# Moving the drive scalings from GpSimd to VectorE, the sine arguments to GpSimd, and splitting two more stores, in a two-layer convolution kernel on one core

## The chip, the core and the metric

The kernel runs on one core of a Trainium2 chip. The core has a matrix engine (TensorE; PE in the profile, with its weight loads as PEld), VectorE (DVE), ScalarE (ACT), GpSimd (POOL) and SyncE (SP), which here only issues DMAs. Each engine works through its own list of instructions in order. All DMAs run on 16 shared DMA engines. DMAs are issued from SP, from ACT (at the start) and from POOL.

The metric is the device time in microseconds. Before the change it is 9159.09 us, the median of three runs from 9153.91 to 9171.87.

## The reference

The input `x` is 8 x 8 x 512 x 512 (batch elements, channels, rows, columns), float32. Two layers are added to it.

```python
# layer 0: spectral convolution of the group-normalised input
x = x + _L0_conv_ref(_gn(x), T, X, weights1_ri, weights2_ri)
#   every second row and column -> rfft2 -> the 4+4 x 4 lowest modes mixed
#   over channels by w1, w2 -> sum with exp(lam * X), exp(lam * T) back to 512 x 512

# layer 1, on v = _gn(x)
grid = drive = v
for _ in range(15):
    mapped = 3.9 * grid * (1.0 - grid)
    local = conv3x3_per_channel(mapped, K_local)
    grid = 0.85 * (0.7 * mapped + 0.3 * local) + 0.15 * drive
cml = clip(grid, 0.0001, 0.9999)
nca = sigmoid(conv1x1(relu(conv3x3(v, Wp, bp)), Wu, bu))     # 8 -> 128 -> 8 channels
gin = concatenate([v, cml, nca])
g   = sigmoid(conv1x1(relu(conv3x3(gin, Wg1, bg1)), Wg2, bg2))
x   = x + g * cml + (1.0 - g) * nca
```

The **drive** is the term `0.15 * drive` in the loop of 15 steps. The sines and cosines of layer 0 are computed in the kernel from `X` and `T`.

## The kernel before

**Planes and slabs.** For each element the normalised input is written to a plane `xn` in DRAM. The 15 steps run on slabs of it: a set (class `Slabs`) holds four channels of four slabs of 32 rows that overlap, as one tile of 128 partitions by 4 x 512. A set loads two drive tiles of that size, `dE` (index 0) and `dO` (index 1), which hold the same rows in two arrangements, since a step turns channels and slabs about. Even steps add `dE`, odd ones `dO`. An element has two halves of four sets each (channels 0 to 3 and 4 to 7), and the second half has a fifth set, the `Tail`. These are two phases of 15 steps: 60 and 75 set-steps, so 135 for an element and 1080 for eight elements.

**One set-step.** `convolve` (L547) issues 48 matmuls from the state `m` into one half of PSUM. `settle` evicts it: VectorE adds the drive (L560, two instructions of 128x1024), ScalarE squares (L566, two). Then `renew` (L593, L594) copies rows that slabs share between the tiles, with small DMAs on GpSimd's queue. PSUM's two halves are used in turn, so the matmuls of one step or round run beside the eviction of the one before.

**The drive scalings.** The drive tiles are scaled in place on GpSimd. `drive(1)` scales `dO` before step 1, in four instructions of 128x512 (L539); it is called by `prepare` (L698) at the start of a turn, as soon as the set's loads were issued in an earlier turn or when the set is due. `drive(0)` scales `dE` after step 1, in one to four instructions (L539, up to 128x2048). After step 13 (`STEPS - 2`) 0.5 is added to `dO` (L570, 128x2048). That is 472 instructions for 72 sets.

**A turn.** `turn` and `work` write out the order by hand, and `keep_order` fixes it on every engine as it stands in the source. A turn has three set-steps, then up to three rounds of the hidden layer (`Hidden.round`: 12 matmuls, counted as 24 in the profile, L746, evicted by ScalarE at L752 and VectorE at L754), then the sums of the hidden layer (L773), and pieces of layer 0 of the next element, and of a gate (class `Gate`). A gate's convolution (L830) is followed by L835 on GpSimd, L836 and L840 on VectorE, the matmuls L847, L851 on ScalarE, L853 on GpSimd and L858 on VectorE. There are 360 such turns, after an opening for the first element and before a closing stretch with hidden rounds and gates alone. Sums and point matmuls of a turn can only start when their evictions are done.

**The opening.** The first element's eight channels are loaded, and layer 0 runs alone: batch statistics (L333), a transform, the sines (`sines`, twelve VectorE instructions of 8x512 at L235 to L238 in three passes, each followed by a sine on ScalarE), the synthesis (L452, L469), the normalisation (L422) and the stores of `xn` (L427). `close(g, ...)` stores two channels for each of the four groups `g`. For the last group of the first element, only the top 16 partitions (64 rows) are stored at first. Then the column tiles of the hidden layer's first rounds are loaded from `xn` (L729), then the drive tiles of the remaining sets of the first phase, and then the rest of the last group (`e.rest`). SyncE issues all of these in this order.

```python
def settle(self, step, ps):
    ...
            if step < STEPS:
                nc.scalar.square(u[:, at], u[:, at])
    if step == 1:
        self.drive(0)
    elif step == STEPS - 2:
        nc.gpsimd.tensor_scalar(d, d, 0.5, None, ALU.add)
    ...
    else:
        self.renew(step)
```

Of the kernel before, what the change touches and what calls it, by code (L numbers as in the profile page):

```python
# [37 lines left out]
ALU = mybir.AluOpType  # L38
# [7 lines left out]
G = 4  # L46
# [3 lines left out]
R, EPS, BETA = 3.9, 0.3, 0.15  # L50
# [4 lines left out]
TICK = 3  # L55
# [16 lines left out]
MAGIC = 12582912.0  # L72
# [47 lines left out]
def conv_layers(ctx: ExitStack, tc: tile.TileContext, a, out):  # L120
    nc = tc.nc
# [9 lines left out]
    class Slots:  # L131
# [4 lines left out]
        def __init__(self, most):  # L136
            self.most, self.held = most, {}
# [24 lines left out]


    put_off, now, rows_due = [], [0], []

    def later(ticks, work):
        put_off.append((now[0] + ticks, work))
# [57 lines left out]
    def sines():  # L225
        u, k, t = (sets.take([8, N], name) for name in ("u", "k", "sines"))
        rd = sm.tile([8, 1], F32, name="rd")
        for to, name, col, shift in (
            (e1[:8], "X", 0, 0.25), (t, "X", 0, 0.0), (e2[:8], "T", 1, waves[:8, 2:3])
        ):  # L230
            xr = grid[name]
            nc.vector.tensor_tensor(rd, xr[:, 2:3], xr[:, 0:1], ALU.subtract)
            nc.vector.reciprocal(rd, rd)
            nc.vector.tensor_tensor(rd, rd, waves[:8, col : col + 1], ALU.mult)
            nc.vector.tensor_scalar(u, xr, rd, shift, ALU.mult, ALU.add)  # L235
            nc.vector.tensor_scalar(k, u, MAGIC, None, ALU.add)
            nc.vector.tensor_scalar(k, k, MAGIC, None, ALU.subtract)
            nc.vector.tensor_tensor(u, u, k, ALU.subtract)  # L238
            nc.scalar.activation(to, u, AF.Sin, scale=6.283185)
        nc.scalar.dma_start(out=e1[8:16], in_=t)  # L240
        for j in range(1, 4):
            nc.scalar.dma_start(out=e2[32 * j : 32 * j + 8], in_=e2[:8])
        for tile_ in (u, k, t, *grid.values()):
            sets.drop(tile_)
# [8 lines left out]
    shift = prep[:, 0:96].rearrange("p (d o) -> p d o", d=3)  # L253
# [68 lines left out]
    def layer0(e, bank):  # L322
# [91 lines left out]
        def close(g, mv):  # L414

            mean, rstd, std = yield from group_stats(mv, 1, bank)
            nc.vector.tensor_copy(means[:, 0, g : g + 1], mean)
            nc.vector.tensor_copy(means[:, 1, g : g + 1], std)
            pair = (2 * g, 2 * g + 1)
            for c in pair:  # L420
                xt = e.x[C + c]
                nc.vector.tensor_scalar(xt, xt, mean, rstd, ALU.subtract, ALU.mult)  # L422

            def rows(lo, hi):
                for c in pair:
                    to = e.xn[1 : N + 1, c].rearrange("(p j) w -> p j w", j=4)
                    nc.sync.dma_start(out=to[lo:hi], in_=e.x[C + c][lo:hi])  # L427

            def rest(lo=TOP):
                rows(lo, P)  # L430
                for c in pair:
                    e.done_with(C + c)

            def store():
                if e.b == 0 and g == G - 1:
                    rows(0, TOP)
                    e.rest = rest
                else:
                    rest(0)
                e.closed.extend(pair)  # L440

            later(1, store)
# [50 lines left out]
    class Slabs:  # L493


        def __init__(self, e, c0, k, above=None):
            self.e, self.c0, self.k, self.above = e, c0, k, above
            self.d, self.m, self.loaded = {}, None, {}

        def channel(self, step, h, t):  # L500
            return self.c0 + (t if step % 2 else h)
# [34 lines left out]
        def drive(self, o):  # L536
            d = self.d[o]
            for lo, hi, add in self.adds(o):
                nc.gpsimd.tensor_scalar(d[:, lo:hi], d[:, lo:hi], BETA, add, ALU.mult, ALU.add)  # L539

        def convolve(self, step, ps):
            m = self.m
# [11 lines left out]
        def settle(self, step, ps):  # L554

            m, d = self.m, self.d[step % 2]
            u = m[:, :, 1 : N + 1]
            for q in range(2):
                at = slice(2 * q, 2 * q + 2)
                nc.vector.scalar_tensor_tensor(  # L560
                    u[:, at], ps[q], FLOOR, d[:, at], ALU.max, ALU.add
                )
                if q:
                    yield
                if step < STEPS:
                    nc.scalar.square(u[:, at], u[:, at])  # L566
            if step == 1:
                self.drive(0)
            elif step == STEPS - 2:
                nc.gpsimd.tensor_scalar(d, d, 0.5, None, ALU.add)  # L570
            elif step >= STEPS - 1:
                sets.drop(d)
            if step == STEPS:
                self.leave()
            else:
                self.renew(step)
# [102 lines left out]
    class Phase:  # L679
# [17 lines left out]

        def prepare(self, n):  # L698
            while self.driven < len(self.sets) and self.ready(self.driven, 1, n):
                self.sets[self.driven].drive(1)  # L700
                self.driven += 1

        def squares(self, n):
            while self.squared < len(self.sets) and sets.room():
# [169 lines left out]
    class Element:  # L874


        def __init__(self, b):
            self.b, self.rows = b, 0
            self.xn, self.cml, self.nca = planes[b % 3]
            self.halves = []  # L880
            for c0 in (0, 4):
                above, half = None, []
                for k in range(SETS):
                    above = Slabs(self, c0, k, above)
                    half.append(above)
                self.halves.append(half)
            self.tail = Tail(self, 0, 0)
            self.past, self.mapped, self.closed = pasts[b % 2], [], []
            self.hidden = Hidden(self)
            self.gates = deque(Gate(self, r) for r in range(0, N, GR))  # L890
            self.back = sm.tile([P, 2], F32, name="back", bufs=3)
            self.x, self.at, self.fetched = {}, {}, 0
            self.bank, self.back_begun = [], False
            self.pieces = layer0(self, self.bank)
            self.need = next(self.pieces)

# [149 lines left out]
    def element(b):  # L1046
        e = Element(b)
        phase(e.halves[0])
        phase(e.halves[1] + [e.tail])
        elements.append(e)  # L1050
        return e

    e = element(0)
# [22 lines left out]
    e.hidden.load()  # L1076
    while first.loads:
        first.load()
    e.rest()

    halves = pairs[:2], pairs[2:]
    used = [0]
# [1 line left out]
    def work(steps, rounds, e, after, gates, transfers, squares=lambda: None):  # L1084

        double = gates == 2 and not others.lag

        def half():
            used[0] += 1
            return halves[used[0] % 2]  # L1090

        settled = iter(())
        for n, (s, step) in enumerate(steps):
            ps = half()
            s.convolve(step, ps)
            next(settled, None)
            settled = s.settle(step, ps)
            next(settled)
            others.finish()
            if gates == 2 and shared.most < 6:  # L1100
                others.load(1)
                gates = 1
        if steps:
            others.finish()
        transfers()
        if steps:
            had = len(others.loaded) + len(others.begun)
            others.load(gates, early=True)
            gates -= len(others.loaded) + len(others.begun) - had
        for _ in range(rounds):  # L1110
            e.hidden.round(half(), after, settled)
        next(settled, None)
        others.finish()
        squares()


        first, second = halves[used[0] % 2], halves[(used[0] + 1) % 2]
        if not others.spectral(WIDE, second):
            used[0] += 1
# [50 lines left out]
    for b in range(B):  # L1170
        e = elements[b]
# [102 lines left out]
```

## Time and profile before

The profile is of one execution of 9170.25 us, of which the span below is 9168.5 us.

| | us | share of the span |
|---|---|---|
| span of the profiled execution | 9168.5 | |
| PE busy | 8748.3 | 95% |
| DVE busy | 5628.9 | 61% |
| ACT busy | 4099.4 | 45% |
| POOL busy | 3383.3 | 37% |
| L547, set-steps, PE (103680 matmuls) | 3681.8 | |
| L746, hidden rounds, PE (24576) | 2779.2 | |
| L560, eviction of set-steps, DVE (2160) | 2543.0 | |
| L754, half of the eviction of rounds, DVE (1024) | 1313.6 | |
| L539, drives, POOL (400) | 367.0 | |
| L570, 0.5 added, POOL (72) | 398.0 | |
| L593 and L594, renewals issued, POOL (3136) | 1689.0 | |

A group of instructions is named by the line of the kernel, its engine and its tiles. Busy time is summed over the instructions of an engine, so it says how much an engine does and not what the others wait for. Where an engine was idle before an instruction, the profile names what released it. An instruction's duration includes the time in which it is held up after its start, so one form at one size can have different durations.

### The profile page before, as it was taken

The page shows a single profiled execution, that of the slowest core. Times are in us where ns is not written, and L with a number is a line of the kernel's source. Part 1 is how long each engine was busy: PE and PEld are TensorE (multiplying, and loading weights), DVE is VectorE, ACT ScalarE, POOL GpSimd, SP SyncE. Part 2 cuts the span into 40 slices and gives each one's busy share as a digit, 9 for nine tenths or more (in the row PEclk, how much of TensorE's full clock was granted, in tenths as well). Part 3 has the DMA queues.
Part 4 walks back from the last instruction along what each step waited for, and adds up shares of the span by engine and source line. Part 5 has one row for each costly group of instructions (what it writes and reads, how often), then busy time and mean ns, then how long its engine had stood idle before and what let it go on. Part 6 is the DMA issues. An engine that isn't in the chain of part 4 may idle for free. (4 is left out here: it accounts for less than half of the span.)

```text
span 9168.5 us, 334776 instructions
## 1 busy us (share of the span) xinstructions
PE 8748.3 (95%) x150992; PEld 4141.6 (45%) x150992; DVE 5628.9 (61%) x5844; ACT 4099.4 (45%) x4285; POOL 3383.3 (37%) x4470
## 2 busy tenths in 40 slices
PE   5999999999999999999999999999999999999999
PEld 2445544444444444444444444444444444444433
DVE  6665567555675567655676556765567655565654
ACT  2455544444444444444444444444444444444432
POOL 3242434324343243433434334343333434454423
PEclk9999999999999999999999999999999999999999
DMA  5241356745566455754557545565465754755587
GB/s 161 81 133 39 108 138 176 171 110 140 145 179 162 112 157 140 186 143 113 155 150 180 140 113 155 155 174 140 113 164 150 180 135 106 177 138 140 118 209 204
DMA packets 695939, 1327.27 MB, mean 145 GB/s; under 512 B 147648, under 2 KB 153152, under 8 KB 667024
## 3 DMA queue, kind: packets, MB, share of 16 engines
q1 hardware_dynamic: 587376, 1235.73, 52.5%
q0 software_dynamic: 104992, 69.33, 3.5%
q8 instruction: 1187, 19.45, 0.9%
q14 instruction: 240, 1.97, 0.1%
q10 hardware_dynamic: 2144, 0.80, 0.0%
HBM read 977.48 MB, written 270.61 MB: 136 GB/s over the span
## 5 line engine op out<-in xcount | busy, mean ns | idle before, releaser
L547 PE MATMUL pair<-m,band 32*32 32x512 f32 x103680 | 3681.8, 604 | 178.4 <-issue 113.3
L566 ACT ACTIVATE m<-m 128x1024 f32<-128x1024 f32 x2016 | 2128.7, 1056 | 2038.6 <-DVE m L560 1963.9
L547 PEld LDWEIGHTS pair<-m,band 32*32 32x32 f32 x103680 | 2141.5, 103 | 1650.2 <-issue 785.9
L746 PE MATMUL pair<-cols,w_p 32*128 32x511 f32 (+1 forms) x24576 | 2779.2, 597 | 22.9 <-DMA cols<-xn 15.1
L754 DVE TENSOR_SCALAR h<-pair,b_p 128x1024 f32<-128x1024 f32 x1024 | 1313.6, 1283 | 1135.9 <-PE pair L746 1125.8
L593 POOL DMA_DIRECT2D m<-m x1568 | 851.0, 543 | 3087.7 <-ACT m L566 3012.8
L746 PEld LDWEIGHTS pair<-cols,w_p 32*128 32x128 f32 x24576 | 1308.8, 185 | 1501.8 <-issue 1157.3
L560 DVE SCALAR_TENSOR_TENSOR m<-pair,dO 128x1024 f32<-128x1024 f32 x1152 | 1356.2, 1219 | 982.0 <-PE pair L547 791.1
L560 DVE SCALAR_TENSOR_TENSOR m<-pair,dE 128x1024 f32<-128x1024 f32 x1008 | 1186.8, 1219 | 862.3 <-PE pair L547 671.3
L752 ACT ACTIVATE h<-pair,b_p 128x1024 f32<-128x1024 f32 x1024 | 1141.1, 1114 | 1184.9 <-PE pair L746 1174.2
L853 POOL TENSOR_TENSOR mix<-mix 96x512 f32<-96x512 f32 x344 | 437.3, 1277 | 1853.1 <-ACT mix L851 1806.1
L773 PE MATMUL pair<-h,w_u 128*32 128x512 f32 x8192 | 996.2, 596 | 72.3 <-DVE y L782 45.7
L830 PE MATMUL pair<-gin,w_g 128*32 128x511 f32 (+1 forms) x8256 | 951.6, 597 | 21.4 <-DMA gin<-nca 11.7
L594 POOL DMA_DIRECT2D m<-m x1568 | 838.0, 534 | 55.1 <-issue 31.7
L773 PEld LDWEIGHTS pair<-h,w_u 128*32 128x32 f32 x8192 | 246.0, 109 | 684.7 <-issue 523.7
L830 PEld LDWEIGHTS pair<-gin,w_g 128*32 128x32 f32 x8256 | 252.5, 110 | 669.5 <-issue 599.0
L785 ACT ACTIVATE y<-y,b_u 128x512 f32<-128x512 f32 x256 | 184.8, 722 | 727.4 <-DVE y L782 727.4
L835 POOL TENSOR_TENSOR mix<-mix 96x512 f32<-96x512 f32 x344 | 443.7, 1292 | 139.6 <-DMA mix<-nca 86.7
L780 ACT COPY y<-pair 128x512 f32<-128x512 f32 x256 | 149.9, 586 | 641.3 <-PE pair L773 622.7
L570 POOL TENSOR_SCALAR dO<-dO 128x2048 f32<-128x2048 f32 x72 | 398.0, 5527 | 95.3 <-DVE m L560 94.4
L847 PE MATMUL pair<-mix,w_g 128*32 128x512 f32 x2064 | 354.4, 601 | 44.1 <-DVE mix L840 40.6
L840 DVE TENSOR_SCALAR mix<-pair,b_g 128x512 f32<-128x512 f32 x344 | 257.1, 747 | 222.6 <-PE pair L830 213.4
(96 smaller groups left out, 3038.9 us busy)
## 6 DMA issues: line engine op xcount, KB each, us to landing
gin<-xn SPq DMA_DIRECT2D x344, 384.0 KB
x<-in_x SPq DMA_DIRECT2D x120, 1024.0 KB
cols<-xn SPq DMA_DIRECT2D x240, 512.0 KB
gin<-cml SPq DMA_DIRECT2D x344, 320.0 KB
gin<-nca SPq DMA_DIRECT2D x344, 320.0 KB
dE<-xn SPq DMA_DIRECT2D x288, 256.0 KB
dO<-xn SPq DMA_DIRECT2D x288, 256.0 KB
mix<-xn SPq DMA_DIRECT2D x344, 192.0 KB
```

What stands on the lines that cost most here:

```text
L547: nc.tensor.matmul(ps[h // 2][32 * t : 32 * t + 32, h % 2], band[at, self.channel(step - 1, h, t), dx], m[at, t, dx : dx + N], start=(n == ...
L560: nc.vector.scalar_tensor_tensor(u[:, at], ps[q], FLOOR, d[:, at], ALU.max, ALU.add)
L566: nc.scalar.square(u[:, at], u[:, at])
L593: nc.gpsimd.dma_start(out=view(tb, rb, dims), in_=view(ta, ra, dims))
L594: nc.gpsimd.dma_start(out=view(ta, ra + s, dims), in_=view(tb, rb + s, dims))
L746: nc.tensor.matmul(ps[g // 2][:, g % 2, lo:hi], w_p[p, dx, i % 2], self.cols[p, i // 2, at : at + hi - lo], start=(n == 0), stop=(n == 2), ...
L752: nc.scalar.activation(h[:, :2], ps[0], AF.Relu, bias=b_p)
L754: nc.vector.tensor_scalar(h[:, 2:], ps[1], b_p, 0.0, ALU.add, ALU.max)
L773: nc.tensor.matmul(ps[32 * g : 32 * g + 32], w_u[:, r % 4], h[:, g], start=(r == hs[0][0]), stop=(r == hs[-1][0]), tile_position=(0, 32 * g),)
L830: nc.tensor.matmul(ps[32 * j : 32 * j + 32, lo:hi], gband[:, dx], gin[:, j, at : at + hi - lo], start=(n == 0), stop=(n == 2), tile_positi ...
L835: nc.gpsimd.tensor_tensor(d, d, ng, ALU.subtract)
L853: nc.gpsimd.tensor_tensor(d, d, mix[: GR * C, 2], ALU.mult)
```

## The change

There are three edits.

1. **Drives on VectorE, kept for the rounds.** `drive` and the addition of 0.5 run on VectorE. They are not issued where they arise but put into a queue `spare`; after each hidden round of a turn one item of it is issued (all four instructions of a `drive(1)` are one item), and what is left is issued after the last round. `prepare` queues a set's `drive(1)` only if its first step is not in this turn; otherwise it is issued right behind the set's first `convolve`.
2. **Sine arguments on GpSimd.** The four 8x512 instructions of each of the three passes in `sines` go to GpSimd. The three short ones before them (`rd`) stay on VectorE.
3. **Split stores.** In the first element the last two groups, that is channels 4 to 7, store only their top 64 rows at first; the rest of all four channels is stored where the rest of two was.

```diff
+    spare = deque()
...
-            nc.vector.tensor_scalar(u, xr, rd, shift, ALU.mult, ALU.add)
-            nc.vector.tensor_scalar(k, u, MAGIC, None, ALU.add)
-            nc.vector.tensor_scalar(k, k, MAGIC, None, ALU.subtract)
-            nc.vector.tensor_tensor(u, u, k, ALU.subtract)
+            nc.gpsimd.tensor_scalar(u, xr, rd, shift, ALU.mult, ALU.add)
+            nc.gpsimd.tensor_scalar(k, u, MAGIC, None, ALU.add)
+            nc.gpsimd.tensor_scalar(k, k, MAGIC, None, ALU.subtract)
+            nc.gpsimd.tensor_tensor(u, u, k, ALU.subtract)
...
             def store():
-                if e.b == 0 and g == G - 1:
+                if e.b == 0 and g >= G - 2:
                     rows(0, TOP)
-                    e.rest = rest
+                    e.rest.append(rest)
...
         def drive(self, o):
             d = self.d[o]
             for lo, hi, add in self.adds(o):
-                nc.gpsimd.tensor_scalar(d[:, lo:hi], d[:, lo:hi], BETA, add, ALU.mult, ALU.add)
+                nc.vector.tensor_scalar(d[:, lo:hi], d[:, lo:hi], BETA, add, ALU.mult, ALU.add)
...
             if step == 1:
-                self.drive(0)
+                spare.append(lambda: self.drive(0))
             elif step == STEPS - 2:
-                nc.gpsimd.tensor_scalar(d, d, 0.5, None, ALU.add)
+                spare.append(lambda: nc.vector.tensor_scalar(d, d, 0.5, None, ALU.add))
...
         def prepare(self, n):
             while self.driven < len(self.sets) and self.ready(self.driven, 1, n):
-                self.sets[self.driven].drive(1)
-                self.driven += 1
+                k, self.driven = self.driven, self.driven + 1
+                if self.at + k >= n + TICK:
+                    self.sets[k].driven = True
+                    spare.append(lambda k=k: self.sets[k].drive(1))
...
-    e.rest()
+    for rest in e.rest:
+        rest()
...
             s.convolve(step, ps)
             next(settled, None)
+            if step == 1 and not s.driven:
+                s.drive(1)
             settled = s.settle(step, ps)
...
         for _ in range(rounds):
             e.hidden.round(half(), after, settled)
+            if spare:
+                spare.popleft()()
         next(settled, None)
+        while spare:
+            spare.popleft()()
```

More of the change, by code (lines that the diff above doesn't have):

```diff
@@ L497, in __init__ @@
             self.e, self.c0, self.k, self.above = e, c0, k, above
-            self.d, self.m, self.loaded = {}, None, {}
+            self.d, self.m, self.loaded, self.driven = {}, None, {}, False
         def channel(self, step, h, t):
@@ L892, in __init__ @@
             self.x, self.at, self.fetched = {}, {}, 0
-            self.bank, self.back_begun = [], False
+            self.bank, self.back_begun, self.rest = [], False, []
             self.pieces = layer0(self, self.bank)
```

## The prediction

> **What bounds the kernel now.** I read the page's first part, then PE's busy time by stretches, then the order of work inside the bad stretches.
>
> ```profile
> span 9168.5 us, 334776 instructions
> ...
> PE 8748.3 (95%) x150992; PEld 4141.6 (45%) x150992; DVE 5628.9 (61%) x5844; ACT 4099.4 (45%) x4285; POOL 3383.3 (37%) x4470
> ```
>
> PE is busy for 8748.3 of 9168.5 us, so a change on DVE or POOL can pay only where it fills PE's idle time, 420 us in all. Where that lies is read from the view of busy time by stretches. Each row is a stretch in us, then PE, PEld, DVE, ACT and POOL busy, the granted clock, the DMA share and GB/s. These four cover one element from the end of its first phase.
>
> ```profile
> 1518.00:1674.00 156.00, 140.51 (x2273) 60.70 (x2264) 97.45 (x87) 67.63 (x69) 83.63 (x86) 0.97 0.78 192
> 1674.00:2123.00 449.00, 443.93 (x7680) 210.73 (x7676) 255.78 (x243) 202.81 (x211) 141.51 (x199) 1.00 0.52 126
> 2123.00:2265.00 142.00, 136.08 (x2502) 68.32 (x2488) 87.69 (x75) 66.45 (x67) 75.25 (x74) 1.00 0.62 160
> 2265.00:2644.00 379.00, 366.58 (x6446) 179.53 (x6442) 266.70 (x321) 175.75 (x192) 115.24 (x178) 0.99 0.57 152
> ```
>
> The first and third rows are the stretches in which the drives are scaled, once at each change of phase. PE idles 156.0 - 140.5 = 15.5 us and 142.0 - 136.1 = 5.9 us there, 21.4 us in 298 us; in the other two it idles 17.5 us in 828 us. At the second rate the 298 us would hold 6.3 us, so the drives' stretches lose about 15 us per element, 8 x 15 = 120 us in the kernel. PE gaps over 0.15 us, summed from the trace over all sixteen such stretches, say 108 us above the rate of the rest. If slowed steps are counted too (from the start of one block of matmuls to the next, over the usual distance), they come to some 190 us. So the prize in the middle is 108 to 190 us at most, for everything that goes wrong at a change of phase.
>
> How POOL's drives do it is seen in the order of time after step 13 (start, length, engine, line, bracket: idle before and its releaser):
>
> ```profile
> 1518.35 5.79 POOL L570 TENSOR_SCALAR dO<-dO 128x2048 f32<-128x2048 f32 x1 [3.65 <-DVE m L560]
> ...
> 1525.26 5.38 POOL L570 TENSOR_SCALAR dO<-dO 128x2048 f32<-128x2048 f32 x1
> ...
> 1531.46 5.38 DVE L836 SCALAR_TENSOR_TENSOR mix<-mix,back 96x512 f32<-96x512 f32 x1
> ...
> 1536.76 0.74 DVE L840 TENSOR_SCALAR mix<-pair,b_g 128x512 f32<-128x512 f32 x1
> ...
> 1537.55 1.51 PE L847 MATMUL pair<-mix,w_g 128*32 128x512 f32 x6 [2.04 <-DVE mix L840]
> ```
>
> L570 of POOL takes 5.4 us and more. L836 of DVE, 0.74 us by its median, needs two SBUF operands and lasts 5.38 us beside it. L840 behind it on DVE is late, so L847 makes PE wait 2.04 us. Thirteen L836 beside an L570 are drawn out so, by 58.5 us in all, and PE has thirteen gaps of over 1 us between L773 and L847, 27 us, one in each of these turns. The same thing at a start of phase:
>
> ```profile
> 1618.90 5.40 POOL L539 TENSOR_SCALAR dO<-dO,base 128x512 f32<-128x512 f32 x8
> ...
> 1621.99 8.12 DVE L858 SCALAR_TENSOR_TENSOR mix<-mix,back 96x512 f32<-96x512 f32 x1
> ```
>
> L858, again 0.74 us alone, holds DVE for 8.12 us beside L539.
>
> **Part 1: drives from POOL to DVE.** POOL loses 72 L570 and 400 L539, 765 us.
>
> ```profile
> L570 POOL TENSOR_SCALAR dO<-dO 128x2048 f32<-128x2048 f32 x72 | 398.0, 5527 | 95.3 <-DVE m L560 94.4
> L539 POOL TENSOR_SCALAR dO<-dO,base 128x512 f32<-128x512 f32 x288 | 214.7, 760 | 403.7 <-DMA dO<-xn 301.8 <-DVE st L469 29.5 <-DVE m L619 22.8
> ```
>
> ```profile
> L619 DVE TENSOR_SCALAR m<-m 128x2048 f32<-128x2048 f32 x72 | 98.0, 1362 | 2.3
> ```
>
> On DVE the nearest rows are L619 (1362 ns) and L422 (1388 ns), both 128x2048 SBUF to SBUF; L236 costs 415 ns at 8x512 and L235 475 ns with a per-partition scalar. So a 128x2048 drive is 1.37 us and a 128x512 one 0.45 us. Sum: (72 + 48) x 1.37 + (288 + 48) x 0.45 + 16 x 1.05 = 332 us. DVE rises from 61% to about 65% and stays below PE.
>
> Which of it is on the path? The instruction lists of the two programs are the same on PE and ACT, and the 472 instructions fall into 188 groups on DVE. I laid each group at its place in the trace.
> - 127 groups stand between two L754 of a turn's rounds. Rounds come every 2.57 us, L754 takes 1.28, so 1.29 us are free against 1.4 to 1.6. The overrun is 0.1 to 0.3 us a time, 41 us over all. PE writes the halves of PSUM in turn, which leaves about 1.3 us before it would wait: I take nothing.
> - 38 groups follow the last round of a turn, some holding two items (2.8 to 4.3 us). Idle DVE time there falls short of them by 55 us. In twenty or so they stand ahead of L836 and L840, so L847 may be late. In twelve of these the 1.4 us replaces 4.6 us of blocking (above: 1531.5 + 1.4 + 0.7 + 0.7 = 1534.4, against 1537.5). In eight, 2.84 us precede an undisturbed L836: about 1 us each. I take 10 us.
> - 23 groups are the second drives of sets that are due, straight before L560. 1.6 us replaces POOL's 2.7 us for the same data, but now DVE itself is held: overrun 8 us, taken as 10 us.
> New waits: a DVE drive(1) waits for its dO load, with every eviction queued behind it. POOL waited 301.8 us for these in 28 cases, at most 19.4 us, but it reached them about a turn earlier. At the DVE places nearly all the loads have landed (the 19.4 us wait ended at 142.4, DVE comes at 147.1). I take 0, with 20 us at the far end. Losses: 20 us.
>
> Gains: the thirteen L847 waits, 27 us; the long gaps behind stacked L570 (3.6 us at 534, 5.9 at 8205, 7.5 at 8659), 17 us; of the remaining 64 us of the 108, what stands near L539 (2 to 5 us gaps such as 2753, 2782, 7845) and behind the renewals L593/L594 that the drives hold up. Some of that belongs to L619, the squares L525 and the loads, which stay. I take half, 32 us, and of the slowed steps (190 - 108 = 82 us) half again, 41 us. Together 117 us, less 20: **-97 us**.
>
> **A rule against it.** L593/L594 are POOL-queue DMAs. Row: two of them ran beside an L619 and took 1.57 and 1.46 us instead of 0.53. The Trainium skill ("SBUF — State Buffer", section "Who interferes with whom") says a DVE `tensor_scalar` in its two-port mode holds the port that GpSimd shares for the whole instruction, and that descriptors written by GpSimd stand still meanwhile. L619's rate, 2048 elements in 1.36 us where L560 takes 1.22 for 1024, fits such a mode, so the new DVE drives can each hold POOL. By the rule, were every lock to reach PE, the 332 us would all be lost; by the rows a renewal is delayed 1 us and is wanted by PE a turn later, and the same lock is held today by POOL's drives for 765 us. I go by the rows: 0, with 30 us at the far end.
>
> **Part 2: sines on POOL.** Between 21.8 and 30.9 us DVE does the twelve sine instructions and waits for ACT between them; then it is the chain to the first synthesis (batch statistics to 46.3, L396 to 57.6, PE follows at once). Still on DVE are three short `rd` triples; the third waits until POOL has read `rd` of the second. POOL has no 8x512 row; L539 (0.68 us at 128x512) and L835 (1.28 us) give 3 x 0.68 + 1.28 = 3.3 us a pass against 2.1. Second pass starts after the first sine (26.1), so DVE is free at 27.3: 3.5 us earlier. The third sine ends near 34 rather than 31.5; ACT's copies behind it (L344) slip by 3 us and have 13 us. Bounds 0 to 4; I take 3.5.
>
> **Part 3: two stores split.** The first round waits for its columns:
>
> ```profile
> 112.24 5.75 SPq L427 DMA_DIRECT2D xn<-x  x4
> 125.83 0.91 SPq L729 DMA_DIRECT2D cols<-xn  x2
> ```
>
> ```profile
> 129.28 10.89 PE L746 MATMUL pair<-cols,w_p 32*128 32x512 f32 x72 [15.11 <-DMA cols<-xn]
> ```
>
> The first row holds four stores, two of 1 MB and two of 128 KB; the columns wait for all. Between 100 and 130 us the DMA engines are busy 0.96 of the time at 250 GB/s. Two 896 KB rests now go behind sixteen loads of dE and dO and ahead of the third column tile, which is issued at 146.0 and first used in the ninth round, at 177.6. By mean rate 1.75 MB are 7 us; by the time from the last dO landing (120.2) to the column issue (125.8) some 4 us. I take 4.5; bounds 2 to 7. Parts 2 and 3 add, since both stand on the one chain to 129.3: **-8 us**.
>
> **Sum.** The profiled run took 9170.25 us (span 9168.5 and 1.75 around it); minus 105 gives 9065. It stands 11 us above the median of three, so the median becomes 9159 - 105 = **9054 us**.
>
> **Rivals.**
> - A, forecast, 60%: 9054, own range 9000 to 9115.
> - B, hidden anyway, 18%: at the starts of phase loads, L619 and L525 hold PE as before; only the L847 waits, the three long gaps and the start come back, 27 + 17 + 8 - 15 = 37 us: 9122. For it: loads are densest there (DMA share 0.78 in the first row). Against: the 8.12 us block of L858.
> - C, deeper, 8%: POOL's drives cause all the slowed steps; 190 + 8 - 10: 8971.
> - D, slower, 9%: the drives ahead of L836/L840 and L560 hold DVE. Place: the last round of a turn. Price: the overruns of all groups, 55 + 41 + 8 = 104 us, none absorbed. It decides once less than that is won back; with 60 us won: 9159 + 104 - 60 = 9203. Against: POOL's blocks of the same L836 go.
> - E, the exchange is even, 5%: 9155. That the edit does nothing is excluded, since the instruction lists show the move.
>
> Range: from C to past B, 8985 to 9140. No change means within 0.2%, 18 us. Faster is A, B and C less a few tails: 0.84; same 0.07; slower 0.09.
>
> **What would show it.** L836 never above 2.1 us (beside L835 only); no 2 us PE gap ahead of L847 after step 13; PE's idle in the stretch of a change of phase down from 15.5 to some 7 us; new DVE rows at 1.37 and 0.45 us; first L746 near 121 us. It is wrong if L847 or L547 wait for DVE more than before, if DVE drives show long waits for dO, or if L593/L594 grow past 1 us.

## The result and the profile after

The changed kernel takes 9107.12 us (median of four runs, 9103.45 to 9110.93) against 9159.55 (four runs of the kernel before, 9153.91 to 9171.87). The ratio is 0.9938, with a 95% interval of 0.9926 to 0.9951: at 9160 us that is a gain of 57 us, give or take 11. The forecast was a gain of 105. The sign is right and the range holds the time, but only half of the forecast gain came. The range, 8985 to 9140 us, is wide enough to hold rival B's time (9122) as well, so that it holds the time says little of the mechanism.

The profiled execution took 9110.93 us. Its page begins:

```profile
span 9109.1 us, 334530 instructions
...
PE 8724.3 (96%) x150992; PEld 4143.7 (45%) x150992; DVE 5843.4 (64%) x6304; ACT 4097.1 (45%) x4285; POOL 2674.7 (29%) x4010
```

PE busy falls from 8748.3 to 8724.3 us for the same matmuls (24 us), and PE's idle time from 420.2 to 9109.1 - 8724.3 = 384.8 us (35 us). POOL falls by 709 us, less than the 765 it gave up, since it took over the sines and its renewals grew longer. DVE rises by 215 us only for 327 us of new work, in the main because L839 (L836 before) and L861 (L858) together are held up 74 us less.

The matmuls take less time because the granted clock is higher. The clock records of the two traces know two values, full and half. Half clock was granted in 41 stretches before, 169 us in all, and in 30 after, 126 us; half of these times, 84 and 63 us, is what PE lost by it. The stretches come with PE's gaps: 40 of the 41 and 29 of the 30 begin in a PE gap of 1.5 us or more or within 2.5 us of its end, and none of the gaps of 1 to 1.5 us, 26 before and 32 after from 140 us on, has one behind it. The gap of 2.04 us that the prediction shows before L847 is an example. Right behind it stands the first row below (kernel before; from:to and length in us, busy times, then granted clock, DMA share, GB/s), with clock 0.50, and the six matmuls of L847 take 1.51 us there. The second row is the same place in the changed kernel, where they take 1.03:

```profile
1538.00:1541.00 3.00, 3.00 (x48) 0.88 (x43) 0.75 (x2) 0.72 (x1) 2.98 (x6) 0.50 0.10 22
```

```profile
1542.00:1549.00 7.00, 7.00 (x140) 2.63 (x147) 3.28 (x8) 2.61 (x4) 1.27 (x1) 1.00 0.51 105
```

So such a gap often costs its own length and 1.7 us more, half of a stretch of 3.4 us. About 20 of the 57 us come in this way, by an estimate from these traces; the other executions agree, with a mean granted clock of 0.993 in the four of the changed kernel and 0.991 in the 61 of the kernel before that ran beside the experiments. That the gaps bring the half clock is read from when it comes; no run sets one without the other.

The view of busy time by stretches, for the same element and the same four parts as before (us from:to and length, then PE, PEld, DVE, ACT and POOL busy, granted clock, DMA share, GB/s):

```profile
1525.00:1677.00 152.00, 140.68 (x2370) 63.82 (x2346) 105.66 (x121) 68.44 (x69) 36.72 (x54) 0.97 0.81 197
1677.00:2127.00 450.00, 442.02 (x7616) 208.97 (x7611) 256.83 (x241) 202.23 (x210) 141.78 (x199) 1.00 0.53 126
2127.00:2261.00 134.00, 130.69 (x2416) 66.77 (x2400) 95.28 (x96) 61.33 (x62) 26.25 (x42) 1.00 0.60 150
2261.00:2642.00 381.00, 370.22 (x6531) 179.58 (x6527) 272.48 (x325) 180.88 (x196) 118.26 (x184) 0.99 0.58 158
```

PE's idle time in the two stretches of a change of phase is now 152.0 - 140.7 = 11.3 and 134.0 - 130.7 = 3.3 us, against 15.5 and 5.9; in the other two 18.8 us, against 17.5. In this element the change brings back 4.2 + 2.6 = 6.8 us there and loses 1.3 elsewhere; the forecast wanted 8.5 in the first stretch alone.

The groups of DVE for the drives in the changed kernel (count, then busy us and mean ns, then idle time before them):

```profile
L540 DVE TENSOR_SCALAR dO<-dO,base 128x512 f32<-128x512 f32 x288 | 119.9, 479 | 3.1 <-DMA mix<-nca 1.7 <-DMA dO<-xn 1.5
L571 DVE TENSOR_SCALAR dO<-dO 128x2048 f32<-128x2048 f32 x72 | 96.3, 1342 | 0.0
...
L540 DVE TENSOR_SCALAR dE<-dE,base_e 128x2048 f32<-128x2048 f32 x48 | 60.0, 1277 | 0.0
L540 DVE TENSOR_SCALAR dE<-dE,base_e 128x512 f32<-128x512 f32 x48 | 35.2, 773 | 0.0
```

The durations of the first two and of the third are close to the forecast 450 and 1370 ns, the 512-wide pieces of `dE` are held up at times, and the sum is 327 us against 332. They hardly wait for loads: 1.5 us for `dO`.

The order of time after step 13 in the changed kernel, in the turn that was shown for the kernel before (start, length, engine and line):

```profile
1536.38 1.22 DVE L571 TENSOR_SCALAR dO<-dO 128x2048 f32<-128x2048 f32 x1
...
1538.95 1.22 DVE L571 TENSOR_SCALAR dO<-dO 128x2048 f32<-128x2048 f32 x1
1539.05 1.21 POOL L595 DMA_DIRECT2D m<-m  x1
...
1541.52 1.22 DVE L571 TENSOR_SCALAR dO<-dO 128x2048 f32<-128x2048 f32 x1
...
1542.65 0.74 DVE L839 SCALAR_TENSOR_TENSOR mix<-mix,back 96x512 f32<-96x512 f32 x1
...
1543.32 0.74 DVE L843 TENSOR_SCALAR mix<-pair,b_g 128x512 f32<-128x512 f32 x1
...
1545.39 1.03 PE L850 MATMUL pair<-mix,w_g 128*32 128x512 f32 x6
```

Each L571 stands behind one L757 and takes 1.22 us. The first two lie between rounds. The third, behind the last round, makes L839 late by about a microsecond, but L839 now lasts 0.74 us instead of 5.38, and L850 has no bracket: PE's wait of 2.04 us is gone. The renewal L595 at 1539.05 takes 1.21 us beside an L571.

What it does at a start of phase is seen in another turn of the changed kernel, in the same view:

```profile
3868.14 0.52 POOL L595 DMA_DIRECT2D m<-m  x1
3868.14 3.04 DVE L540 TENSOR_SCALAR dE<-dE,base_e 128x512 f32<-128x512 f32 x2
...
3868.67 1.29 POOL L838 TENSOR_TENSOR mix<-mix 96x512 f32<-96x512 f32 x1
...
3872.30 2.46 DVE L540 TENSOR_SCALAR dE<-dE,base_e 128x2048 f32<-128x2048 f32 x2
...
3874.69 0.74 DVE L839 SCALAR_TENSOR_TENSOR mix<-mix,back 96x512 f32<-96x512 f32 x1
...
3875.35 0.74 DVE L843 TENSOR_SCALAR mix<-pair,b_g 128x512 f32<-128x512 f32 x1
...
3876.14 1.06 PE L850 MATMUL pair<-mix,w_g 128*32 128x512 f32 x6 [1.64 <-DVE mix L843]
```

The second row is an item of two L540 between rounds, one of 512 and one of 1536 columns; L595 and then L838 of POOL run beside it, and the short one lasts 2.11 us instead of 0.48. The fourth row is two items behind the last round, two L540 of 2048 columns. They take 2.46 us ahead of L839 and L843, and PE waits 1.64 us at L850. So a part of the wait that the change removes after step 13 comes back at the starts of phases. The waits of the whole execution say how much of it. The view of waits lists who waited for whom: us in all, times, the longest. Before:

```profile
PE pair L847 <- DVE mix L840: 40.6, 26, 3.7
```

After:

```profile
PE pair L850 <- DVE mix L843: 33.1, 22, 3.8
```

The wait that the change was to remove fell by 7.5 us only. Of gaps over 1 us between the sums and this matmul there were 13 with 26.9 us, each in a turn after a step 13. Those are gone, and nine with 18.2 us are new. Six of the nine, 9.4 us, stand behind L540 at a start of phase: five of 1.63 or 1.64 us, like the one above, and one of 1.19. The other three, 8.9 us, have no scaling in front of them. They follow L571 in the last element, where only one or two rounds stand in a turn and two or three items come behind the last of them:

```profile
8584.64 3.48 DVE L571 TENSOR_SCALAR dO<-dO 128x2048 f32<-128x2048 f32 x3
...
8590.50 1.73 PE L850 MATMUL pair<-mix,w_g 128*32 128x512 f32 x6 [3.59 <-DVE mix L843]
```

The same three, of 1.96, 3.60 and 3.31 us, stand in the run without scalings (no_drives, below). They are a price of moving the 0.5, and the prediction did not have it.

Which turns won and which lost is found by following the start of PE's first matmul of each turn through both traces. The differences, summed over the eight elements (an element has 45 turns; single executions, so some us are chance):

| | after, less before (us) |
|---|---|
| the opening, up to the first set-step | -5.6 |
| turns 0 to 6 and 20 to 27, the starts of the two phases | +22.2 |
| turns 15 to 19 and 40 to 44, behind step 13 | -75.6 |
| all other turns | -1.2 |

So the forecast gain behind step 13 came in full, and more; by the clock records 24 us of it are PE time that half clock no longer takes in these turns. The forecast gain at the starts of phases did not come: these became slower, 3 us of it by the clock.

### The profile page after: what moved, and what is told of

The parts are those of the page before. It is cut to its first block, busy times and chain, and to the rows that moved or that the text cites. A ratio compares the mean times of both kernels' runs of the same rounds, so it can differ in the third digit from the quotient of the medians.

```text
span 9109.1 us, 334530 instructions
## 1 busy us (share of the span) xinstructions
PE 8724.3 (96%) x150992; PEld 4143.7 (45%) x150992; DVE 5843.4 (64%) x6304; ACT 4097.1 (45%) x4285; POOL 2674.7 (29%) x4010
## 3 DMA queue, kind: packets, MB, share of 16 engines
q14 instruction: 239, 1.96, 0.1%
## 5 line engine op out<-in xcount | busy, mean ns | idle before, releaser
L594 POOL DMA_DIRECT2D m<-m x1568 | 863.4, 551 | 4137.5 <-ACT m L567 4078.9
L757 DVE TENSOR_SCALAR h<-pair,b_p 128x1024 f32<-128x1024 f32 x1024 | 1313.4, 1283 | 971.5 <-PE pair L749 953.2
L595 POOL DMA_DIRECT2D m<-m x1568 | 861.0, 549 | 53.8 <-issue 26.4
L838 POOL TENSOR_TENSOR mix<-mix 96x512 f32<-96x512 f32 x344 | 444.1, 1294 | 142.4 <-DMA mix<-nca 81.6
L843 DVE TENSOR_SCALAR mix<-pair,b_g 128x512 f32<-128x512 f32 x344 | 257.0, 747 | 204.2 <-PE pair L833 193.7
L850 PE MATMUL pair<-mix,w_g 128*32 128x512 f32 x2064 | 352.7, 598 | 36.7 <-DVE mix L843 33.1
L839 DVE SCALAR_TENSOR_TENSOR mix<-mix,back 96x512 f32<-96x512 f32 x344 | 311.3, 905 | 30.7 <-DMA mix<-nca 21.3
```

The lines of the kernel that those rows point to most:

```text
L594: nc.gpsimd.dma_start(out=view(tb, rb, dims), in_=view(ta, ra, dims))
L595: nc.gpsimd.dma_start(out=view(ta, ra + s, dims), in_=view(tb, rb + s, dims))
L757: nc.vector.tensor_scalar(h[:, 2:], ps[1], b_p, 0.0, ALU.add, ALU.max)
L838: nc.gpsimd.tensor_tensor(d, d, ng, ALU.subtract)
```

## The experiments

The theory after the result: moving the 0.5 wins nearly all, taking the scalings (`drive`) off POOL wins little since loads and squares hold the starts of phases, and the new scalings on DVE cost about as much as they win, mostly behind the last round of a turn. The rival: POOL's scalings did cost what the forecast said, and the new places on DVE give it back. Each kernel was timed in five rounds, in alternation with the kernel before; us are the ratio's difference from 1 times 9160.

| kernel | edit in a few words | median us | ratio, 95% interval | us |
|---|---|---|---|---|
| h_only | only the 0.5 to DVE | 9116.44 | 0.9948, 0.9934 to 0.9962 | -48 ± 13 |
| drives_only | only the scalings to DVE | 9167.6 | 1.0004, 0.9994 to 1.0013 | +4 ± 9 |
| start_only | only sines and stores | 9161.73 | 0.9999, 0.9989 to 1.0008 | -1 ± 9 |
| no_drives | after, scalings left out | 9078.11 | 0.9906, 0.9892 to 0.9919 | -86 ± 12 |
| no_drives_before | before, scalings left out | 9143.15 | 0.9983, 0.9972 to 0.9993 | -16 ± 10 |
| hybrid | after, scalings on POOL | 9106.51 | 0.9943, 0.9928 to 0.9958 | -52 ± 14 |
| at_once | after without the queue | 9140.41 | 0.9979, 0.997 to 0.9988 | -19 ± 8 |
| tail_pop | after, rest of the queue issued later | 9091.19 | 0.9924, 0.991 to 0.9937 | -70 ± 12 |
| tail_due | tail_pop, due sets on POOL | 9087.58 | 0.9914, 0.9901 to 0.9928 | -79 ± 13 |
| tail_nostart | tail_pop, old sines and stores | 9094.16 | 0.9923, 0.9912 to 0.9935 | -71 ± 11 |
| tail_no_drives | tail_pop, scalings left out | 9074.83 | 0.99, 0.9887 to 0.9913 | -92 ± 12 |
| ahead15 | after, loads issued earlier | 9132.89 | 0.9964, 0.995 to 0.9978 | -33 ± 13 |

### One part at a time

**h_only**, on the kernel before:

```diff
             elif step == STEPS - 2:
-                nc.gpsimd.tensor_scalar(d, d, 0.5, None, ALU.add)
+                spare.append(lambda: nc.vector.tensor_scalar(d, d, 0.5, None, ALU.add))
...
             e.hidden.round(half(), after, settled)
+            if spare:
+                spare.popleft()()
         next(settled, None)
+        while spare:
+            spare.popleft()()
```

> Only the addition of 0.5 after step 13 moves to VectorE, through the queue behind the rounds; the two scalings stay on GpSimd, sines and stores as before. Theory 1 (all that the middle gained comes from the turns around step 13, and moving the two scalings won nothing or cost a little): 60 to 75 us under the kernel before, so at or under the changed kernel, about 9090. Theory 2 (both kinds of drive gave about half of the gain each, as the prediction's sum has it): 25 to 30 us under before, about 9130.

Measured: -48 ± 13, between the ranges of the two theories. This one move of 72 instructions is, within the intervals, the whole change. The waits of this kernel (its lines stand one further down; the profiled execution, 9131 us, is among its longer ones):

```profile
PE pair L848 <- DVE mix L841: 21.8, 14, 3.7
```

Without the scalings on DVE this wait falls from 40.6 to 21.8 us; with them it stands at 33.1. The three gaps of the last element, 8.9 us, are in the 21.8.

**drives_only**: the changed kernel with the 0.5 on GpSimd, where it was, and with the sines and stores as before.

```diff
             elif step == STEPS - 2:
-                spare.append(lambda: nc.vector.tensor_scalar(d, d, 0.5, None, ALU.add))
+                nc.gpsimd.tensor_scalar(d, d, 0.5, None, ALU.add)
```

> The two scalings (drive(0), drive(1)) move to VectorE with the queue and the due rule; the addition of 0.5 stays on GpSimd, sines and stores as before. Theory 1: between 0 and 25 us slower than before, 9160 to 9185. Theory 2: 20 to 30 us faster, about 9135.

Measured: +4 ± 9, as theory 1 had it: no gain that can be told from none. Four hundred instructions and 367 us of POOL's work changed their engine for nothing.

**start_only**: edits 2 and 3 alone, as in the diff above, on the kernel before.

> Sine arguments on GpSimd and the split stores alone. Both theories: the first step 5 to 6 us earlier, and the whole run earlier by that, 9154. If the opening's shift is taken back later, no difference.

Measured: -1 ± 9. In its trace the first set-step starts 5.9 us earlier (in h_only, without these edits, 1.0 us earlier, so a part is chance). The opening wins some us, and the interval of the total is too wide to find them. The three parts add up: -48 + 4 - 1 = -45, beside -57 ± 11.

### What the scalings cost on either engine

**no_drives** (and **no_drives_before**, with `nc.gpsimd` in the line taken out):

```diff
             for lo, hi, add in self.adds(o):
-                nc.vector.tensor_scalar(d[:, lo:hi], d[:, lo:hi], BETA, add, ALU.mult, ALU.add)
+                pass
```

> The changed kernel with the 400 scaling instructions of drive(0) and drive(1) left out, so the drives are not scaled. Theory 1a (what the starts of phase could have given back is eaten by the new VectorE instructions): 25 to 60 us under the changed kernel, 9050 to 9080. Theory 1b (the starts of phase are held by the loads of the drive tiles, so the scaling costs nothing on either engine): within 10 us of the changed kernel, 9097 to 9107.

> The kernel before with the 400 scaling instructions left out (drives not scaled), the addition of 0.5 still on GpSimd. This is the most that taking the scalings off GpSimd can win. Prediction's sum: 73 us for the waits near the scalings, so about 9087. Theory 1 (the scalings cost about 30 us on either engine, the rest of the starts of phase is held by other things): 15 to 40 us under before, 9120 to 9145.

Measured: -86 ± 12 for no_drives, as theory 1a had it, and -16 ± 10 for no_drives_before, as theory 1 had it and far from the 73 of the prediction's sum. The scalings on DVE cost 86 - 57 = 29 us, ± 17 (the two half widths, squared and added). On POOL they cost the kernel before 16 ± 10, and this is all that taking them off POOL could win in that kernel. Both are the same to within their errors, which fits drives_only. In no_drives_before the wait ahead of the same matmul is nearly as before (40.6 us):

```profile
PE pair L847 <- DVE mix L840: 37.4, 22, 3.8
```

and a turn after step 13 is in the order of time as it was in the kernel before:

```profile
1539.79 5.37 DVE L836 SCALAR_TENSOR_TENSOR mix<-mix,back 96x512 f32<-96x512 f32 x1
...
1540.95 5.38 POOL L570 TENSOR_SCALAR dO<-dO 128x2048 f32<-128x2048 f32 x1
...
1545.08 0.74 DVE L840 TENSOR_SCALAR mix<-pair,b_g 128x512 f32<-128x512 f32 x1
...
1545.87 1.06 PE L847 MATMUL pair<-mix,w_g 128*32 128x512 f32 x6 [2.03 <-DVE mix L840]
```

L836 still takes 5.37 us and PE still waits 2.03 us, with no scaling anywhere. The blocking at step 13 needs no L539.

**hybrid** is the changed kernel with the scalings on GpSimd at their old places:

```diff
-                nc.vector.tensor_scalar(d[:, lo:hi], d[:, lo:hi], BETA, add, ALU.mult, ALU.add)
+                nc.gpsimd.tensor_scalar(d[:, lo:hi], d[:, lo:hi], BETA, add, ALU.mult, ALU.add)
...
-                spare.append(lambda: self.drive(0))
+                self.drive(0)
...
-                k, self.driven = self.driven, self.driven + 1
-                if self.at + k >= n + TICK:
-                    self.sets[k].driven = True
-                    spare.append(lambda k=k: self.sets[k].drive(1))
+                self.sets[self.driven].drive(1)
+                self.driven += 1
```

> Scalings on GpSimd as before, the addition of 0.5 on VectorE through the queue, sines and stores as in the changed kernel. Theory 1 (the scalings cost about the same on either engine, some 30 us): within 12 us of the changed kernel, 9098 to 9116. Theory 2 (VectorE is the better home by 25 us or more, as the prediction's sum has it): 9130 or more.

Measured: -52 ± 14, the same as the changed kernel, as theory 1 had it. Against no_drives the scalings on POOL cost 86 - 52 = 34 ± 18 us here, with the 0.5 on DVE; this does not differ from the 16 ± 10 beyond the errors.

### Where on DVE they stand

**at_once** is the kernel before with sines and stores as in the change, and both kinds of drives on DVE at the places in the source where POOL's were, with no queue:

```diff
-                nc.gpsimd.tensor_scalar(d[:, lo:hi], d[:, lo:hi], BETA, add, ALU.mult, ALU.add)
+                nc.vector.tensor_scalar(d[:, lo:hi], d[:, lo:hi], BETA, add, ALU.mult, ALU.add)
...
-                nc.gpsimd.tensor_scalar(d, d, 0.5, None, ALU.add)
+                nc.vector.tensor_scalar(d, d, 0.5, None, ALU.add)
```

> All drives on VectorE at the places where GpSimd had them (start of a turn, inside the settling of a step), without the queue; sines and stores as in the changed kernel. If it matters that the items lie between the rounds: 30 to 120 us slower than the changed kernel, 9140 to 9230, since each item (1.3 to 1.9 us) then stands ahead of an eviction of a step. If VectorE has room anywhere: 9107.

Measured: -19 ± 8, so the queue is worth about 33 us by the medians (9140 against 9107). The group of the `dO` scalings in at_once shows the likely reason:

```profile
L539 DVE TENSOR_SCALAR dO<-dO,base 128x512 f32<-128x512 f32 x288 | 120.2, 483 | 105.2 <-DMA dO<-xn 64.1 <-DMA mix<-nca 40.7
```

DVE waits 64.1 us for the loads of `dO` there, with every eviction behind it, where it waits 1.5 us in the changed kernel. POOL waited 301.8 us for them in the kernel before and had no eviction behind it. No run parts this wait from the items' place ahead of evictions.

**tail_pop** issues the queue behind the first two rounds only, and what is left at the end of the turn's point matmuls instead of ahead of L839:

```diff
-        for _ in range(rounds):
+        for n in range(rounds):
             e.hidden.round(half(), after, settled)
-            if spare:
+            if spare and n < 2:
                 spare.popleft()()
         next(settled, None)
-        while spare:
-            spare.popleft()()
...
         others.spectral(LAST, [first[1][:, 0]])
+        while spare:
+            spare.popleft()()
```

> The changed kernel, but the queue is emptied behind the first two rounds of a turn only, and what is left is issued at the end of the turn, behind the gate's VectorE work. If the items behind the last round, ahead of the gate's L839 and L843, are what costs most of the 29 us that the scalings cost on VectorE: 10 to 20 us under the changed kernel, about 9090. If the drives of due sets or the sheer VectorE time cost it: within 5 us of it.

Measured: 9091.19, -70 ± 12. The turn whose L850 waited 1.64 us, in tail_pop's order of time:

```profile
3863.29 0.73 DVE L839 SCALAR_TENSOR_TENSOR mix<-mix,back 96x512 f32<-96x512 f32 x1
...
3863.95 0.74 DVE L843 TENSOR_SCALAR mix<-pair,b_g 128x512 f32<-128x512 f32 x1
...
3864.61 2.46 DVE L540 TENSOR_SCALAR dE<-dE,base_e 128x2048 f32<-128x2048 f32 x2
...
3865.31 1.03 PE L850 MATMUL pair<-mix,w_g 128*32 128x512 f32 x6
```

The 2.46 us of L540 now come behind L843, and L850 starts with no wait. Over the execution:

```profile
PE pair L850 <- DVE mix L843: 15.1, 15, 3.8
```

18 us of this wait are gone against the changed kernel, and no gap over 1 us is left between the sums and this matmul. By the nine gaps above, half of that is the scalings' and half the L571's of the last element. The time goes with it: 16 us by the medians. The intervals of the two ratios overlap, so the gain over the changed kernel is shown in the wait more firmly than in the time.

**tail_no_drives** is tail_pop with the scalings left out.

> tail_pop with the 400 scaling instructions left out (drives not scaled). If the late place has hidden nearly all of what the scalings cost on VectorE: within 8 us of tail_pop, 9083 to 9091. If the time that is left comes from the drives of due sets and the crowded rounds: 12 to 20 us under it, 9071 to 9079.

Measured: -92 ± 12, by the medians 16 us under tail_pop, as the second case had it. In tail_pop the scalings still cost 92 - 70 = 22 ± 17 us, beside 29 ± 17 in the changed kernel.

**tail_due** takes the 23 `drive(1)` of due sets, which stand straight ahead of an eviction, back to GpSimd at the start of the turn:

```diff
                     spare.append(lambda k=k: self.sets[k].drive(1))
+                else:
+                    self.sets[k].driven = True
+                    self.sets[k].drive(1, nc.gpsimd)
```

> tail_pop with the second drives of due sets (23 groups) issued on GpSimd at the start of the turn, as before the change. If these groups, which stand on VectorE between two evictions, cost time: 5 to 15 us under tail_pop, 9076 to 9086. If GpSimd's 2.7 us for the same data is on the path instead of VectorE's 1.7 us: 9091 to 9110.

Measured: -79 ± 13, by the medians 4 us under tail_pop, less than the first case and not told apart from none.

**tail_nostart** is tail_pop with sines and stores as in the kernel before.

> tail_pop with sines and stores as in the kernel before. If the opening's 5 us reach the end: 9094 to 9098. If they are taken back: 9091.

Measured: -71 ± 11 against -70 for tail_pop; the medians are 3 us apart, 9094 against 9091. This does not tell the two cases apart.

### What holds the starts of phases

**ahead15** issues the loads of the drive tiles earlier, in the changed kernel:

```diff
-AHEAD = 12
+AHEAD = 15
```

> The changed kernel with the drive tiles of a phase asked for three set-steps (one turn) earlier, where there is room for them. If the starts of phase are held by the loads of the drive tiles and the squares behind them (theory 1b): 10 to 40 us under the changed kernel. If they are held by something else, or no room comes free earlier: within 10 us of it or slower, since the gates pause a turn earlier too.

Measured: -33 ± 13, so 24 us slower than the change by the ratios. `AHEAD` also sets when gates pause, and the run moved both; it says nothing clean on the loads. What speaks for them is the view of waits: ScalarE's wait at the squares for the load of `dE`, before, after and in no_drives:

```profile
ACT m L525 <- DMA dE<-xn: 51.8, 10, 7.6
```

```profile
ACT m L526 <- DMA dE<-xn: 46.7, 8, 7.7
```

```profile
ACT m L526 <- DMA dE<-xn: 51.5, 9, 7.3
```

It hardly moves, wherever the drives are scaled or whether they are. And without any scalings, the starts of phases in no_drives are shorter than before by 13.4 us only, by the same count of turns as above. That these loads and squares are what holds them is argued from the traces, not shown by a run.

## Why the prediction was right or wrong

**Right in sign, because of step 13.** The sum had 27 us for the thirteen waits of L847 and 17 us for the long gaps behind stacked L570. h_only measures -48 ± 13 for just this move. The chain that the prediction read, L570 beside L836, then L840, then L847, is what the traces of h_only and no_drives_before show from both sides. That the sum, 44 us, comes so near has luck in it. The thirteen waits went. Of the three long gaps, that of 3.6 us at 534 stayed: it stands in the changed kernel at 529.02 with 3.42 us and no L571 beside it. The other two went, 13.4 us, and the three gaps behind L571 in the same element, 8.9 us, came. In return there were the 24 us by the clock in these turns, which the sum did not name.

**The step that failed: "I take half, 32 us, and of the slowed steps half again, 41 us".** These 73 us were ascribed to the scalings L539 and to the renewals that they hold up. no_drives_before measures everything that POOL's scalings cost: 16 ± 10 us. The reading behind the 73, one L858 drawn out to 8.12 us beside L539, was true, and it was taken for a cost to PE without following who waited for that L858. The step ascribed half the disorder of a change of phase to its most visible instruction, though the prediction itself named L619, L525 and the loads as what stays. And of the 82 us of slowed steps, some 50 are half clock, by an estimate: so much the clock records give for the sixteen stretches before. With POOL's scalings left out some 44 of them remain, in the changed kernel 34. What holds the starts of phases otherwise stays open.

**The losses, 20 us, were somewhat small.** The scalings on DVE cost 29 ± 17 us. The place was named right, the last round ahead of L836 and L840, and the size too: 10 us for eight groups, where the trace shows six new gaps of 9.4 us behind scalings. The three gaps behind L571 come on top and were not foreseen. Where the rest of the 29 us arises, and whether "I take nothing" for the groups between rounds was right, no run shows. So the exchange of L539 was 16 against 29 where the forecast had 73 against 20. The rise at the starts of phases, +22 us by turns, is in part these six gaps.

**Part 2, 3.5 us forecast.** The pass on POOL was sized from two-operand rows at 3.3 us. It takes 4.9 in the changed kernel's order of time:

```profile
21.08 0.68 POOL L236 TENSOR_SCALAR u<-X,rd 8x512 f32<-8x512 f32 x1 [9.18 <-DVE rd L235]
...
21.85 1.51 POOL L237 TENSOR_SCALAR k<-u 8x512 f32<-8x512 f32 x1
...
23.45 1.49 POOL L238 TENSOR_SCALAR k<-k 8x512 f32<-8x512 f32 x1
25.02 1.25 POOL L239 TENSOR_TENSOR u<-u,k 8x512 f32<-8x512 f32 x1
...
28.34 4.82 DVE L334 BATCH_NORM_STATS2 st<-x 128x6 f32<-128x512 f32 x8
```

L237 and L238 take 1.5 us each at 8x512, twice L236. DVE was free at 28.3, not 27.3; the third sine starts at 38.3 where it started at 30.9 before. The batch statistics reach PE at 46.84 against 47.45, but their first instruction had started 0.8 us earlier too, since the loads of `x` landed earlier in this execution. So nothing of the 3.5 us is left. L334 above starts 2.5 us earlier than before, but L288, eight short copies behind it, takes 3.11 us beside the sines on GpSimd where it took 1.52, and L262, just before, 0.56 where it took 0.18.

**Part 3, 4.5 us forecast.** The rows of SP's queue and of PE's first round in the changed kernel:

```profile
111.36 4.48 SPq L428 DMA_DIRECT2D xn<-x  x4
120.56 0.92 SPq L732 DMA_DIRECT2D cols<-xn  x2
```

```profile
124.15 10.44 PE L749 MATMUL pair<-cols,w_p 32*128 32x512 f32 x72 [12.10 <-DMA cols<-xn]
```

The second row is the columns' load: issued at 120.56 against 125.83, and PE starts at 124.15 against 129.28. That is 5.1 us, of which 0.8 had come with the loads of `x`; the 4.3 left are the stores', close to the forecast. "Near 121" had used the sum of both parts. The intervals of start_only and tail_nostart are too wide to find 4 or 5 us in the total.

**The rule against it.** The renewals did grow beside DVE's drives: L594 and L595 take 863.4 + 861.0 = 1724 us against 851.0 + 838.0 = 1689, and 31 of 3136 last over 1 us, 24 of them beside an L571, against two before. That is the sign which the prediction had called a sign of error, but PE does not wait for them: the view of waits has 8.3 us of PE waits for renewed rows before and 2.1 after. The row, a delay of 1 us that PE does not wait for, decided, not the 332 us that the rule would cost if every lock reached PE. That DVE's `tensor_scalar`s hold renewals, as the rule says, these 24 show.

**The other signs.** "L836 never above 2.1 us" was wrong: its longest is 3.21 us, nine are above 2.1, each beside two or more POOL instructions in a row, such as L838 twice. But none of 344 is over 4 us, against twelve before, and its busy time falls from 372.2 to 311.3 us. The waits for `dO` at the new places were 1.5 us, forecast 0.

**Of the rivals**, B had the mechanism in the main: of the middle, what comes back is behind step 13. Its 9122 is 15 us above the time and the forecast's 9054 is 53 us below. A was right on the cause for step 13 and wrong for the starts of phases. C, which had POOL's drives cause all slowed steps, falls with no_drives_before (and its own 8971 lay outside the range that was said to run from C). D had the place right at a price of 18 us instead of 104.

## What to carry to other kernels

Before work is moved off an engine, ask what the kernel wins if that work is not there at all: one run with it left out gives the most that any place can win, and here it was 16 ± 10 us against 73 ascribed. An instruction drawn out by a shared resource costs only if its consumer is late, so follow each to the engine that sets the end; L570 was such a case and L539 hardly. Count with each gap of the bounding engine what its clock does right behind it. When work is put into an in-order queue, its place decides: the same drives on DVE differ by some 50 us between their old places in DVE's list (9140) and behind the point matmuls (9091).

## What the runs showed of the hardware

- GpSimd is slow in one form of `tensor_scalar`. With a single operation and a constant (L237, L238) it takes 1.48 to 1.51 us at 8x512, with two operations and a per-partition scalar (L236) 0.68 us. The same holds at 128x2048: L570 with its single addition of 0.5 takes 5.4 us, 2.6 ns for each of the 2048 elements of a partition, where a `dE` scaling of that size on GpSimd, with two operations, takes 1.98 us. On DVE both take 1.22 to 1.28 us. Part of L570's harm may thus be its form; an addition with two operations on GpSimd was not tried.
- A VectorE instruction can be held through several GpSimd instructions in a row. The L839 of 3.21 us ends only after the two L838 of 1.29 and 1.28 us beside it, and the 128x512 scaling at 3868.14, 0.48 us by its median, lasts 2.11 us beside L595 of 0.52 us, which starts with it, and L838 of 1.29 us.
- Short DVE copies suffer too: the eight copies of L288 in the opening take 3.11 us beside the sines on GpSimd, 1.52 before.
- Half clock follows gaps of PE: in the kernel before, from 140 us on, 41 of the 84 gaps of 1.5 us or more, and 36 of the 57 of 2 us or more, have a stretch of half clock begin in them or within 2.5 us of their end; of the 26 gaps between 1 and 1.5 us none has. A stretch lasts 3.4 us or a multiple of it, but for the one that the end of the program cuts.
